# A graph layer as one stream: late rows and root parts beside the first half of the block steps, tiles finished one by one beside the second half

## The chip, the core and the metric

The kernel runs on one core of a Trainium2 chip. The metric is the time of one execution on the device, in microseconds (us). The engines of the core are PE (TensorE, matmul), DVE (VectorE), ACT (ScalarE), POOL (GpSimd, which issues the gathers here) and SP (SyncE, which issues the plain transfers).

## The reference

The input is x (1250 rows of 512 numbers) and 41,250 edges sorted by target (20,000 random pairs in both directions, and one loop at every node). Two graph layers run one after the other, then a mixture of experts:

```
def _graph_conv_max(x, src, dst, W_rel, b, W_root):
    agg = jax.ops.segment_max(x[src], dst, num_segments=N)
    agg = jnp.where(jnp.isfinite(agg), agg, 0.0)
    return agg @ W_rel.T + b + x @ W_root.T
...
h = relu(_graph_conv_max(layernorm(x), src, dst, W1_rel, b1, W1_root))
h = relu(_graph_conv_max(h, src, dst, W2_rel, b2, W2_root))
x = x + h
x = x + ffn(layernorm(x))
```

In the ffn, softmax(rows @ Wr) over all rows picks 512 rows for each of 8 experts (top-k); each expert is two matmuls with a gelu between, and its result, times the probability, is added to its rows.

## The kernel before

**Tiles.** The 1250 rows are 10 tiles of 125 rows (one row a partition). A table of all rows lies in DRAM (table_d, one for each layer). The maximum over a node's neighbours is taken in three ways that add up:

- **Block steps** (`block_steps`, L582). For every tile t and every block b of 125 source rows, the first two neighbours of each row that lie in block b are fetched by matmul: one-hot matrices (`ohs`) times the block's rows, which lie in SBUF as three bf16 parts (`xh`). That is 6 matmuls into a PSUM tile `pq` (two buffers), then one DVE maximum of 125x1024 into `acc2` (for b = 0 an ACT copy). 10 x 10 = 100 steps make a layer; after a tile's tenth step its result is folded into `acc`.
- **Own rows** (`own`, L478). Seven more neighbours of each row, by indirect DMA from POOL (`hb<-table_d,nat_i`), 125 rows of 2 KB each, into `hb` (four buffers of four gathers each; `gathers`, L444), joined by DVE maxima (`merged`, L456, `joined`, L659).
- **Late rows** (`late_groups`, L672). Rows with still more neighbours are sorted into ten lists with 34, 15, 12, 11, 9, 8, 7, 5, 4 and 2 neighbours: 107 gathers in 30 groups of up to four (`hb<-table_d,late_i`). Each list's result goes to DRAM (`late_d`, shown as ovf_d) and comes back to its rows by one gather for each tile (`back`, `hb<-ovf_d,slot_i`), which waits until all lists are stored.

**Root parts** (`root_part`, L314): a tile's row times W_root, plus b: read from table_d, transposed on PE, one bias matmul and four 128x512 f32 matmuls, in six pieces; the result goes to root_d in DRAM. **Convolution** (`conv`, L689): the joined maxima, transposed (`turned`), times W_rel, plus the root part by an identity matmul: five f32 matmul pairs in a row.

**Order.** Every engine keeps the order in which the code records its instructions (`InOrder`, L24; this is why nearly all rows of the profile carry the line L34, and groups are told apart by their tiles). So the order of the loops below is the order of each engine's queue, and an engine that waits holds up all that it has behind it.

A layer is two phases. `first_phase` (L612) runs the block steps with the 60 root pieces spread over all 100 steps, and spreads groups of gathers over them: a group's gathers are recorded ahead, its merge when a computed number of steps is done (`due`). In layer 0 these are the 30 late groups and the own groups of tile 3 (tiles 0 to 2 were joined earlier); in layer 1 the late groups and those of tiles 0 to 3. `second_phase` (L723) has no block steps: own rows of tiles 4 to 9, the back gathers four tiles at a time, and for every two tiles the transposes, convolution and end of tile. The end of a tile in layer 0 is `hidden` (L696): relu, store to the next table, split into the three bf16 parts. In layer 1 it is `residual` (L704): relu and add x, layernorm, store, transpose into `yT`, router logits. Five block steps of layer 1 stand in layer 0's second phase (`begun`, L794), when `xh` of the first five blocks is ready.

The expert part (`Routing`, L1169, and `expert_choice`, L1346) begins with some of expert 0's first matmuls, done for all rows (`dense_steps`, L1285, in three cuts of 4, 3 and 3 tiles, the first two kept in PSUM until the softmax is done), and finds the threshold of the 512 best rows in eight rounds (L1420), each a count on DVE, a small matmul `pn` and a step.

Of the kernel before, what the change touches and what calls it, by code (L numbers as in the profile page):

```python
# [18 lines left out]
P = 128  # L19
# [22 lines left out]
def fast_gnn(tc, ctx, sh, io, y_d):  # L42
# [154 lines left out]
    def load_root(layer):  # L197
        wroot = gw.tile([P, KC, D], F32, name="wroot", bufs=1)
        sp.dma_start(wroot, io[f"w{layer + 1}_root_t"].rearrange("(c p) n -> p c n", p=P))
        brow = gw.tile([1, D], F32, name="brow", bufs=1)  # L200
        sp.dma_start(brow, io[f"b{layer + 1}"])
        weights[layer][:2] = wroot, brow
# [111 lines left out]
    def root_part(layer, t):  # L314
# [3 lines left out]
        turned(rows_ahead.pop(t)[:TN], hT)  # L318
        if t + 3 < NT:
            fetch_row(layer, t + 3)  # L320
        else:
            fetch_root(layer, t + 3 - NT)
# [161 lines left out]
    EARLY = 4  # L484
# [120 lines left out]
    ROOT_PIECES = 2 + KC  # L605
    BEFORE = 4
# [5 lines left out]
    def first_phase(layer, lead, groups, lists, blocks, done):  # L612

        roots = in_turn([root_part(layer, t) for t in range(NT)])
        n_steps, given = NT * NB, 0
        def step():
            nonlocal done, given
            if layer == 0 and done % NB == 4 and done // NB + 2 < NT:  # L620
                onehots(done // NB + 2)
            if layer == 0 and done == NB + 2:
                own_early(2)
            next(blocks)
            done += 1
            while given < done * ROOT_PIECES * NT // n_steps:
                next(roots, None)
                given += 1
            next(blocks)

        while done < lead:
            step()
        for n, (rows, i, fresh, whole) in enumerate(groups):
            due = lead + BEFORE + (n_steps - lead - BEFORE) * n // len(groups)
# [7 lines left out]
            while done < due:  # L642
                step()
# [10 lines left out]
        while done < n_steps:  # L654
            step()
        for _ in roots:
            pass
# [4 lines left out]

    def own_groups(layer, tiles):
        groups = []
        for t in tiles:
            parts_ = grouped(own(layer, t))
            for k, rows in enumerate(parts_):
                whole = (lambda aw, both, t=t: joined(aw, t)) if k + 1 == len(parts_) else None
                groups.append((rows, None, k == 0, whole))
        return groups  # L670
# [24 lines left out]

    def hidden(t, pm):  # L696
        row = gk.tile([P, D], F32, name="line", bufs=LINES)
        act.activation(row[:TN], pm[:TN], AF.Relu)
        stored(table_d[1][t * BR:t * BR + BN, :], row)
        fetch_root(0, t + 3)  # L700
        r1 = gk.tile([P, D], F32, name="line", bufs=LINES)
        yield from parts(t, row[:TN], r1[:TN])

    def residual(t, pm):  # L704
        xt = x_tiles[t % 6]
        fetch_root(1, t + 3)
        fetch_x(t + 3)
        yield
        dve.scalar_tensor_tensor(acc[:TN, t, :], pm[:TN], 0.0, xt[:TN], op0=ALU.max, op1=ALU.add)
        moments(t)  # L710
        spread(t, t + 1)
        yield
        inverted(t, t + 1)
        yn = gk.tile([P, D], F32, name="line", bufs=LINES)
        normed(t, yn[:TN])
        stored(y_d[t * TN:(t + 1) * TN, :], yn)
        yield
        turned(yn[:TN], yT[:, :, t * TN:(t + 1) * TN])
        yield
        head.logits(t, ps_t.tile([P, KC, P], F32, name="pt").rearrange("p c n -> p (c n)"))  # L720
        yield

    def second_phase(layer, finish, beside):  # L723

        going, turns = [], {}

        def on():
            for g in list(going):  # L730
                if next(g, True):
                    going.remove(g)

        def own_rest(t):
            aw = wide()
            for k, rows in enumerate(grouped(own(layer, t))):
                merged(gathers(rows), aw, k == 0)
            joined(aw, t)

        def backs(tiles):  # L740
            hb, _ = gathers([(late_d, slot_i[:, t:t + 1]) for t in tiles])
            for k, t in enumerate(tiles):
                dve.tensor_max(acc[:TN, t, :], acc[:TN, t, :], hb[:TN, k, :])

        def turn(t):
            turns[t] = gk.tile([P, KC, TN], F32, name="turn", bufs=3)
            turned(acc[:TN, t, :], turns[t])

        def ended(*tiles):
            for t in tiles:  # L750
                if t not in turns:
                    turn(t)
                if t + 1 in ready:
                    turn(t + 1)
                g = finish(t, conv(layer, t, turns.pop(t)))
                next(g)
                on()
                going.append(g)

        own_rest(4)  # L760
        backs((0, 1, 2, 3))
        ready = (0, 1, 2, 3)
        own_rest(5)
        ended(0, 1)
        own_rest(6)
        ended(2, 3)
        backs((4, 5, 6, 7))
        ready = (4, 5, 6, 7)
        own_rest(7)
        ended(4, 5)  # L770
        own_rest(8)
        ended(6, 7)
        own_rest(9)
        beside()
        backs((8, 9))
        ready = (8, 9)
        if layer == 1:
            head.constants()
            head.begin(4)
        ended(8, 9)  # L780
        while going:
            on()
            if layer == 1:
                head.begin(1)

    first_phase(0, 6, late_groups(0) + own_groups(0, range(KEPT, EARLY)), set(),
                block_steps(set(range(KEPT))), 0)
# [3 lines left out]
    ready_steps = 5  # L791
    blocks = block_steps(set())

    def begun():  # L794
        load_root(1)
        for _ in range(2 * ready_steps):
            next(blocks)

    second_phase(0, hidden, begun)
    for t in range(3):  # L800
        fetch_row(1, t)
    first_phase(1, 10, late_groups(1) + own_groups(1, range(EARLY)), set(range(NT)), blocks, ready_steps)

    head = Routing(tc, sh, ohs.rearrange("p t n -> p (t n)").bitcast(F32)[:, KC * N:],
                   xh.rearrange("p t k d -> p (t k d)").bitcast(F32), yT)
    head.wide = lambda: ps_q.tile([P, R, D], F32, name="pq")
    x_tiles = [head.left[:, k * D:(k + 1) * D] for k in range(6)]

    def fetch_x(t):
        if t < NT:  # L810
            sp.dma_start(x_tiles[t % 6][:TN], x[t * TN:(t + 1) * TN, :])

    for t in range(3):
        fetch_x(t)
    second_phase(1, residual, lambda: None)
# [353 lines left out]
class Routing:  # L1169
# [4 lines left out]
    def __init__(self, tc, sh, spare, spare2, yT):  # L1174
# [10 lines left out]
        def take(n, dtype=F32, of=spare):  # L1185
# [8 lines left out]
        self.prob = take(N)  # L1194
        self.tops = take(NT)
        self.sm = take(4)
        self.alike = take(P)
# [10 lines left out]
        self.dense = [(take(KC * F).rearrange("p (c f) -> p c f", c=KC),  # L1208
                       take(FC * D).rearrange("p (c d) -> p c d", c=FC)) for e in range(DENSE)]

        self.left = spare[:, self.taken:]
# [4 lines left out]
        self.waiting = []  # L1216
        self.steps = self.dense_steps()
        sp.dma_start(self.wr_s, sh["wr"].rearrange("(c p) e -> p c e", p=P))

    @staticmethod  # L1220
    def words(sh):
# [3 lines left out]
        return (KC * E + KC * P + N + NT + 4 + P + E + 9 + 2 * CC + 3 * P // 2 + NT * E * 5 // 2 + E * FC  # L1225
                + DENSE * (KC * F + FC * D)), FC * N + DENSE * NT * D

    def constants(self):
        dve, act, pe, pool, sp = self.engines
        fw1, fw2 = self.sh["fw1"], self.sh["fw2"]  # L1230
        E, R = fw1.shape[0], self.R
        NT = len(self.sh["rows"])
        sp.dma_start(self.fb1_s, self.sh["fb1_t"])
        for e, (w1, w2) in enumerate(self.dense):
            sp.dma_start(w1, fw1[e].rearrange("(c p) f -> p c f", p=P))
            sp.dma_start(w2, fw2[e].rearrange("(c p) d -> p c d", p=P))
# [30 lines left out]
    def logits(self, t, pl):  # L1267
# [7 lines left out]
        for c in range(KC):  # L1275
            pe.matmul(pl[:, :r], self.wr_rep[:, c].rearrange("p e r -> p (e r)"),
                      self.yT[:, c, t * TN:t * TN + r], start=(c == 0), stop=(c == KC - 1))
        act.copy(self.prob[:, t * TN:t * TN + r], pl[:, :r])
# [6 lines left out]
    def dense_steps(self):  # L1285
# [6 lines left out]
        for e in range(DENSE):  # L1292
            w1, w2 = self.dense[e]
            for n, (t0, t1) in enumerate(zip(cuts, cuts[1:])):
                c0, w = t0 * TN, sum(rows[t0:t1])
                early = e == 0 and n < 2
                if early:
                    both = self.wide()
                for f in range(FC):
                    ph = both[:, f, :] if early else self.bank()  # L1300
# [20 lines left out]
    def softmax(self):  # L1321
# [9 lines left out]
        self.begin(8)  # L1331
# [3 lines left out]
    def begin(self, n):  # L1335

        for _ in range(n):
            if len(self.waiting) < 2 * self.FC:
                next(self.steps)
# [6 lines left out]
def expert_choice(tc, ctx, sh, xs, yT, y_d, out, head):  # L1346
# [73 lines left out]
    for i, shift in enumerate(SHIFTS):  # L1420
# [7 lines left out]
        if i == 0:  # L1428

            for t in range(NT):  # L1430
# [4 lines left out]
        else:  # L1435
# [195 lines left out]
def gnn_expert_choice_kernel(  # L1631
# [49 lines left out]
    with tc.For_i(0, n_again, 1):  # L1681
        with ExitStack() as st:
# [3 lines left out]
            first, second = (spool.tile([P, n], F32, name=f"spare{k}") for k, n in enumerate(Routing.words(both)))  # L1686
            head = Routing(tc, both, first, second, yT)
            head.constants()
            with tc.tile_pool(name="lps", bufs=2, space=PSUM) as lps:
                for t in range(len(both["rows"])):  # L1690
                    head.logits(t, lps.tile([P, D], F32, name="pl"))
                head.wide = lambda: lps.tile([P, 2, D], F32, name="pw")
# [50 lines left out]
```

## Time and profile before

| | us |
|---|---|
| median of 9 runs (lowest, highest) | 922.07 (918.48, 927.66) |
| the profiled execution | 919.23 |
| its span in the profile | 917.4 |
| set-up, to the first late gather | 0 to 113.1 |
| layer 0, first phase | 113.1 to 318 |
| layer 0, second phase, to the first gather of layer 1 | 318 to 399.8 |
| layer 1, first phase | 399.8 to 610.4 |
| layer 1, second phase, to the last logits | 610.4 to 721 |
| softmax, threshold, experts | 721 to 917.4 |

The busy shares over the span are PE 78%, DVE 69%, POOL 56%, ACT 17%. The borders in the table are read from the timeline: 113.1 and 399.8 are the first late gather of each layer, 318 and 610.4 the last fold of each layer's block steps, 721 the last maximum over the logits. A row of the timeline gives the start, the time from the first start to the last end of the merged instructions, the engine, the operation with its output and inputs, the count, and in brackets how long the engine had been idle and what ended that.

### The profile page before, as it was taken

To read this page: it belongs to the slowest core of one execution; us is meant where nothing else is said; L and a number is where in the kernel's file an instruction comes from. 1 tells how busy PE (TensorE), PEld (TensorE's weight loads), DVE (VectorE), ACT (ScalarE), POOL (GpSimd) and SP (SyncE) were. 2 spreads that over 40 slices of the span, in tenths; PEclk is the share of its full clock that TensorE was granted. 3 is DMA by queue.
4 is the path that set the end of the run, shared out by engine and by line. 5 is a ranking of instruction groups with operands and counts; after the bars stand their busy time and mean duration, and the time that the engine had idled before them with its cause. 6 is when DMAs were issued, how large, how long until landed. Compare 5 with 4: busy or idle time off the path is not lost. (4 is left out here: it accounts for less than half of the span.)

```text
span 917.4 us, 8453 instructions
## 1 busy us (share of the span) xinstructions
PE 715.9 (78%) x2554; PEld 377.2 (41%) x2554; DVE 630.2 (69%) x1154; ACT 158.6 (17%) x283; POOL 517.3 (56%) x535
## 2 busy tenths in 40 slices
PE   0193568898989798679888899858859588999992
PEld 0141334454545443335444445433434444444440
DVE  6899489998998866528998989997541565233210
ACT  0641000000000133120000101000311612212110
POOL 6544777776556677046777677777710301466542
PEclk9997879999999989789998999988969889999997
DMA  7587568877667678356877877778850504677753
GB/s 187 160 245 205 137 194 173 212 209 245 188 209 211 209 230 279 130 162 184 182 248 235 267 232 233 229 216 253 261 183 11 174 0 158 140 185 173 136 101 49
DMA packets 70376, 170.57 MB, mean 186 GB/s; under 512 B 13014, under 2 KB 17684, under 8 KB 70322
## 3 DMA queue, kind: packets, MB, share of 16 engines
q0 software_dynamic: 37472, 114.19, 46.8%
q1 hardware_dynamic: 32030, 54.66, 18.9%
q10 hardware_dynamic: 820, 1.10, 0.5%
q8 instruction: 22, 0.36, 0.2%
q14 instruction: 32, 0.26, 0.1%
HBM read 141.46 MB, written 28.40 MB: 185 GB/s over the span
## 5 line engine op out<-in xcount | busy, mean ns | idle before, releaser
L34 PE MATMUL pq<-xh,ohs 126*125 126x512 bf16 x1200 | 296.6, 391 | 64.2 <-DVE acc L34 62.3
L34 POOL DMA_INDIRECT hb<-table_d,late_i x214 | 226.4, 1058 | 131.4 <-issue 51.9
L34 PEld LDWEIGHTS <-ohs 126*125 126x125 bf16 (+1 forms) x1221 | 167.0, 139 | 217.0 <-issue 145.1
L34 DVE TENSOR_TENSOR acc<-acc,pq 125x1024 f32<-125x1024 f32 x180 | 219.2, 1218 | 47.6 <-PE pq L34 41.0
L34 POOL DMA_INDIRECT hb<-table_d,nat_i x140 | 145.6, 1040 | 60.6 <-issue 34.7
L34 PE MATMUL pm<-wrel,turn 128*125 128x512 f32 x160 | 81.4, 656 | 8.9 <-DVE acc L34 6.3
L34 PE MATMUL pm<-wroot,turn 128*125 128x512 f32 x160 | 86.7, 624 | 0.0
L34 ACT COPY acc<-pq 125x1024 f32<-125x1024 f32 x20 | 20.3, 1014 | 357.0 <-PE pq L34 357.0
L34 DVE TENSOR_TENSOR wide<-wide,hb 125x1024 f32<-125x1024 f32 (+1 forms) x60 | 71.4, 1190 | 1.8
L34 POOL DMA_INDIRECT ysel<-y_d,idx x28 | 27.6, 988 | 75.1 <-issue 32.0
L34 DVE TENSOR_TENSOR hb<-hb 125x1024 f32<-125x1024 f32 (+2 forms) x55 | 52.6, 957 | 17.9 <-DMA hb<-table_d,nat_i 17.9
L34 POOL DMA_INDIRECT out<-oo,idx x28 | 44.8, 1600 | 15.8 <-DVE oo L34 8.1
L34 PE MATMUL pm<-yselT,w 128*128 128x512 f32 x112 | 49.9, 599 | 4.7 <-ACT yselT L34 4.7
L34 PE MATMUL pm<-w,hT 128*128 128x512 f32 x112 | 52.7, 591 | 0.0
L34 PEld LDWEIGHTS pm<-wrel,turn 128*125 128x125 f32 x160 | 31.8, 208 | 48.0 <-issue 39.6
L34 DVE TENSOR_TENSOR wide<-hb 125x1024 f32<-125x1024 f32 (+1 forms) x40 | 48.0, 1199 | 5.1 <-DMA hb<-table_d,nat_i 5.0
L34 DVE TENSOR_SCALAR oo<-pm,val 128x512 f32<-128x512 f32 x28 | 21.0, 751 | 44.0 <-PE pm L34 44.0
L34 PEld LDWEIGHTS pm<-wroot,turn 128*125 128x125 f32 x160 | 31.8, 199 | 11.0 <-issue 2.5
L34 ACT COPY turn<-pt 128x500 f32<-128x500 f32 x40 | 22.8, 574 | 68.0 <-PE pt L34 67.7
L34 DVE COPY got<-pi 128x20 f32<-128x20 f32 x7 | 1.2, 178 | 47.7 <-PE pi L34 47.7
L34 PEld LDWEIGHTS pm<-yselT,w 128*128 128x128 f32 x112 | 20.7, 190 | 29.8 <-issue 23.4
L34 DVE TENSOR_REDUCE ohs<-ohs 128x1 f32<-128x125 f32 (+1 forms) x11 | 3.0, 272 | 41.1 <-ACT ohs L34 41.1
(236 smaller groups left out, 785.7 us busy)
## 6 DMA issues: line engine op xcount, KB each, us to landing
w<-in_fw SPq DMA_DIRECT2D x14, 512.0 KB
ohs<-idx_d SPq DMA_DIRECT2D x10, 615.2 KB
ahead<-table_d SPq DMA_DIRECT2D x20, 250.0 KB
root_d<-line SPq DMA_DIRECT2D x20, 250.0 KB
ahead<-root_d SPq DMA_DIRECT2D x20, 250.0 KB
ovf_d<-line SPq DMA_DIRECT2D x18, 224.0 KB
hb<-table_d,late_i POOLq DMA_INDIRECT x214, 6.0
ohs<-in_x SPq DMA_DIRECT2D x10, 250.0 KB
```

The lines of the kernel that those rows point to most:

```text
L34: made = call(*args, **kwargs)
```

## The change

- **Blocks** is now a class that holds a layer's 100 steps and its root pieces. The root pieces are spread over the first `during` steps only: 50 in layer 0, 55 in layer 1 (there from the steps already done on).
- **first_part** takes the place of first_phase: lead steps (8 in layer 0, before 6), then the 30 late groups alone, spread over the steps up to `during`. No own groups are in it.
- **last_part** takes the place of second_phase. It counts ticks. Each tick records one block step (as long as there are any; after that a piece of other work, `beside`), then starts a tile if its start tick has come, and records one piece of every tile begun: merge of its first four gathers; merge of the other four (the back gather is one of them) and join; a tick with nothing; transposes; convolution; and the end of the tile in one to five further pieces. A tile's eight gathers are recorded when the tile before it starts. The start ticks are 0, 4, 7, 10, 14, 20, 26, 32, 38, 43 in layer 0 (tile 3 first, then 0, 1, 2, 4 and on) and 0, 4, 9, 13, 17, 22, 26, 30, 35, 39 in layer 1.
- The split into bf16 parts leaves `hidden`. It is done for all ten tiles by `next_layer`, after layer 0's last block step, with up to nine steps of layer 1 between.
- In layer 1 the root parts read the hidden rows from `acc` in SBUF rather than from DRAM.
- W_root lies in another pool, and its place is used for expert 0's weights after layer 1's root parts; these are loaded at tick 0 of layer 1's last part. x, the router's weights and its constants move to other places with later loads; three x tiles are held where there were six.
- All three cuts of expert 0's first matmuls are now made before the softmax, one half column at a time in ticks without block steps. The ten transposes of the probabilities move from the threshold's round 0 to rounds 1 and 2 (five each), in which no such matmuls stand now.

The core of the diff:

```
     def root_part(layer, t):
...
-        turned(rows_ahead.pop(t)[:TN], hT)
-        if t + 3 < NT:
+        turned(rows_ahead.pop(t)[:TN] if layer == 0 else acc[:TN, t, :], hT)
+        if layer == 0 and t + 3 < NT:
             fetch_row(layer, t + 3)
-        else:
-            fetch_root(layer, t + 3 - NT)
+        elif t + 3 >= NT:
+            fetch_root(layer, order[layer][t + 3 - NT])
...
+        def step(self, roots=True):
...
+            next(self.steps)
+            self.done += 1
+            while roots and self.given < (self.done - self.base) * ROOT_PIECES * NT // (self.during - self.base):
+                next(self.roots, None)
+                self.given += 1
+            next(self.steps)
...
+    def first_part(layer, blocks, lists):
+        groups = late_groups(layer)
+        lead = blocks.done + BEFORE
+        if layer:
+            blocks.base = blocks.done
         for n, (rows, i, fresh, whole) in enumerate(groups):
-            due = lead + BEFORE + (n_steps - lead - BEFORE) * n // len(groups)
+            due = lead + (blocks.during - lead) * n // len(groups)
...
     def hidden(t, pm):
-        row = gk.tile([P, D], F32, name="line", bufs=LINES)
-        act.activation(row[:TN], pm[:TN], AF.Relu)
-        stored(table_d[1][t * BR:t * BR + BN, :], row)
-        fetch_root(0, t + 3)
-        r1 = gk.tile([P, D], F32, name="line", bufs=LINES)
-        yield from parts(t, row[:TN], r1[:TN])
+        act.activation(acc[:TN, t, :], pm[:TN], AF.Relu)
+        stored(table_d[1][t * BR:t * BR + BN, :], acc[:, t, :])
+        ready.add(t)
+        yield
...
+        def tile_work(k):
+            t = order[layer][k]
+            got = fetched.pop(t)
+            if layer == 0 and t < KEPT:
+                dve.tensor_max(acc[:TN, t, :], acc[:TN, t, :], got[0][:TN, t, :])
+            else:
+                aw = wide()
+                merged(got[0], aw, True)
+                yield
+                merged(got[1], aw, False)
+                while blocks.done < (t + 1) * NB:
+                    yield
+                joined(aw, t)
+            yield
+            if not blocks.over():
+                yield
+            hT = gk.tile([P, KC, TN], F32, name="turn", bufs=3)
+            turned(acc[:TN, t, :], hT)
+            yield
+            pm = conv(layer, t, hT)
+            if k + 3 < NT:
+                fetch_root(layer, order[layer][k + 3])
+            yield
+            yield from finish(t, pm)
+
+        fetch(0)
+        begun = tick = 0
+        while begun < NT or going:
+            if not blocks.over():
+                blocks.step(roots=False)
+            else:
+                beside()
+            if tick in at:
+                at[tick]()
+            if begun < NT and tick >= starts[begun]:
+                fetch(begun + 1)
+                going.append(tile_work(begun))
+                begun += 1
             for g in list(going):
                 if next(g, True):
                     going.remove(g)
+            tick += 1
...
+    first = Blocks(0, set(range(KEPT)), 50)
...
+            second = Blocks(1, set(), 55)
+        for t, g in splits.items():
+            if next(g, True):
+                whole.add(t)
...
+        if second.done < NB - 1 and second.done in whole:
+            second.step(roots=False)
...
+    last_part(0, first, (0, 4, 7, 10, 14, 20, 26, 32, 38, 43), hidden, {5: lambda: load_root(1)}, next_layer)
+    while len(whole) < NT:
+        next_layer()
+    first_part(1, second, set(range(NT)))
...
+    last_part(1, second, (0, 4, 9, 13, 17, 22, 26, 30, 35, 39), residual, {0: head.load_dense, 5: begun}, dense)
     head.softmax()
...
-        if i == 0:
-            for t in range(NT):
+        if i in (1, 2):
+            for t in range(NT // 2) if i == 1 else range(NT // 2, NT):
...
-        else:
+        elif i:
             beside()
```

## The prediction

> **What bounds the kernel now.** First the busy time of each engine by stage (columns: stretch, its length, then busy us and count of PE, PEld, DVE, ACT, POOL, then PE's clock, DMA share, GB/s); the stretches are those of the table above.
>
> ```profile
> 113.10:318.00 204.90, 175.33 (x684) 97.19 (x683) 187.01 (x209) 19.28 (x28) 136.20 (x129) 0.96 0.73 206
> 318.00:399.80 81.80, 63.86 (x176) 30.22 (x176) 49.24 (x65) 23.91 (x41) 39.62 (x37) 0.90 0.62 191
> 399.80:610.40 210.60, 185.03 (x704) 101.09 (x704) 184.50 (x172) 19.65 (x29) 155.08 (x149) 0.96 0.77 227
> 610.40:721.00 110.60, 86.19 (x291) 47.17 (x292) 56.08 (x122) 23.44 (x55) 47.08 (x63) 0.86 0.54 171
> ```
>
> In the first phases DVE is busy 91% and 88%, PE 86% and 88%: both are the bound, and their queues mesh. The second phases have no full engine: PE 78%, DVE 60% and 51%. They are what the change goes for: 82 + 111 us in which block steps could run.
>
> Second, the timeline, for how far PE runs ahead of DVE:
>
> ```profile
> 604.51 1.02 PE L34 MATMUL pm<-wroot,turn 128*125 128x512 f32 x2
> ...
> 605.79 0.69 DVE L34 TENSOR_TENSOR acc<-acc,wide 125x512 f32<-125x512 f32 x1
> ...
> 606.40 2.54 DVE L34 TENSOR_TENSOR acc<-acc,pq 125x1024 f32<-125x1024 f32 x2
> ...
> 607.67 1.46 PE L34 MATMUL pq<-xh,ohs 126*125 126x512 bf16 x6 [2.13 <-DVE acc L34]
> ```
>
> PE stands idle 2.13 us until the first of two maxima (606.40 + 1.22) is done: with two pq buffers PE is at most two steps ahead, and while DVE joins own rows PE stops. Third, the price of a gap in PE:
>
> ```profile
> 376.97 5.23 PE L34 MATMUL pq<-xh,ohs 126*125 126x512 bf16 x12 [4.49 <-DVE acc L34]
> ...
> 391.50 3.60 PE L34 MATMUL pm<-wrel,turn 128*125 128x512 f32 x8
> 394.94 1.02 PE L34 MATMUL pm<-ahead,ident 125*125 125x512 f32 x2
> 395.80 0.38 PE L34 MATMUL pq<-xh,ohs 126*125 126x512 bf16 x1
> ```
>
> Twelve step matmuls take 5.23 us after a gap of 4.49, and 2.75 elsewhere (415.88). A convolution is 395.80 - 391.50 = 4.3 us of PE in one piece.
>
> **Prices from rows.** Block step on PE 2.75/2 less overlap = 1.30; maximum on DVE 1.22, 1.27 to the next. Merge of the first four gathers 1.26, of the second four 2.5 (two operations), fold and join 0.7 each. Four transposes 0.45 and ACT copy 0.6; end of tile in layer 1 on DVE 0.69 + 0.69 + 0.18 + 0.15 = 1.8 with gaps, then 0.35, ACT 0.8; logits 0.9. Gathers: 1.25 back to back in quiet stretches (399.81, 401.06); in 560 to 600, 31 in 40 us, so 1.29. I take 1.30; the mean busy of 1.058 plus 0.30 of issue, 1.36, is the upper end.
>
> **First parts.** 107 late gathers now have 38 steps (layer 0) and 42 (layer 1), where 114 and 135 had some 90. POOL needs 107 x 1.30 = 139 us. PE there: 42 steps x 1.30 + ten root parts x 4.7 (five pairs of 0.86 and the transposes) = 102; DVE some 125 (layer 0: 38 maxima, 60 us of late merges, lists, one-hots). So **POOL becomes the bound**, which it was not. The layer 0 part starts at 113.1 as before: the two more lead steps fill a 7.25 us wait of DVE for the lists. POOL ends at 252. Then the last gather must land (6.3), be merged and stored, and the back gather of the first tile waits for that store, lands (6.4) and is merged at tick 1: 11 us until tick 0 in effect, 263.
>
> **Last part of layer 0.** I walk one tile at six ticks' spacing through the two queues, time from the first maximum. DVE: max 0 to 1.25, merge to 2.5, max to 3.8, merge to 6.2, join to 7.6, two max to 10.1. PE: third step at 1.3, fourth at 3.8 (each frees with a maximum two before), transposes wait for the join, 7.6; fifth step waits for a maximum, 8.9 to 10.2; convolution to 14.5; then two steps to 17.1, and DVE, idle since 11.7 but for one maximum, starts the next tile at **17.3**. Work was 12.5 on either engine: the join stops PE 3 us and the convolution stops DVE 4. The first 14 ticks (cheap tiles 0 to 2) take 42 us, four tiles 69, the last five-tick one 16, then seven maxima, merges and the join of tile 9, 15, transposes to relu 6: 148. Stored 3.2 us later (as 396.6 to 399.81 now), the gathers of layer 1 start at 263 + 148 + 3 = 414, now 399.8: **+14**.
>
> **The seam.** Ten splits (20 subtractions of 0.69) and eight maxima, with four lead steps, hold DVE until about 440; POOL has filled its four buffers at 414 + 21 = 435 and waits 5, as it now does at 424.35 (4.83). So 414 + 5 + 139 + 11 = 569 at tick 0 of layer 1's last part.
>
> **Last part of layer 1.** A loop carries it: maximum, end of the tile before (1.8), merge 2.5, join 1.4, maximum, 0.35, ACT normalization 0.8: 9.5; then on PE its transposes and the tile's own 0.9, step 1.3, logits 0.9, convolution 4.3, step 1.3 and the way to DVE: 9.1. **18.6** at four ticks, where PE has 11.3 of work and DVE 12.7. Walking all start ticks (five-tick rounds 23 to 25, the four-tick rounds after them 13) sets ticks 9, 22, 35 at 34, 89, 146, and 39 at 160; tile 9 then needs its steps, join, transposes, convolution between halves of expert 0's columns, normalization and logits: 34. So 569 + 194 = 763, now 721: **+42**. Before, the same 45 steps cost 45 x 2.2 and the second phase 111, together 210 with four tiles' own rows in the steps: the stream saves some 16 there, and the crammed first part has spent three times that.
>
> **Routing and gaps.** In the second threshold round pn waits behind ten transposes: 728.35 to 736.38 is 8.0, later rounds 2.57. Split in two they hide mostly under the count (1.5): -4. Expert 0's third cut, 8 half columns of which about five are left, delays the first pn by 1 to 2: net -2, taken between -6 and +6. The weights of expert 0, for which PE waited 7.56 at 686.86, come at tick 0: hidden behind forty ticks. The walk above ran PE at full clock, but it has gaps of 4 to 7 us in nearly every layer 1 round, beyond those that slowed the rows above (3.35 before 636.82 already did: 5.37 for the eight wrel matmuls against 3.60). Cost of one: 5.37 - 3.60 = 1.8, up to 2.5 from the twelve. I count it for about half of nine rounds, +8, because a cold stretch can fall where DVE is the later one; none and 22 are the ends.
>
> The Trainium skill, "TensorE: Matmul & The Clock Gate", section "HAM oscillation — how this bites in real kernels", warns against PE gaps over about 3.4 us, which then recur each round; that speaks against this order, in which a join and a convolution alternate. Its section "What's actually happening" puts the ramp at under 1% of a typical kernel's span; by that the term would be at most 9 us here, by the rows up to 22, and the trace shows for itself that a gap of 2.13 us costs nothing and one of 4.49 does.
>
> **Sum** against the profiled execution, 919.2: +42 (which holds layer 0's +14) - 2 + 8 = 967; the median of the runs lies 2.8 above the profiled one, so **969**. Bounds: gathers at 1.25 give -5 a layer, at 1.36 +6; gaps 0 or 22.
>
> **Rivals.**
>
> *Rival 1, faster: the queues mesh as in the first phase.* If the stream runs with 9% stalls (DVE 187 of 205), layer 0's last part is PE's 50 x 1.30 + 47 = 112, /0.91 = 123, and 9 of tail: gathers at 398. Layer 1: 398 + 155 + (45 x 1.30 + 60 + 9 of early columns)/0.91 + 12 = 705. That is -16, routing -2: 901, with the median 904. For it: second phases at 60% DVE. Against: the 4.3 us convolution in one piece and two pq buffers. It decides from rounds some 3 us shorter than my walk (15.5 for 18.2, 14.5 for 17.3): fifteen rounds x 3 = 45.
>
> *Rival 2, slower still: gaps keep PE cold and transfers slow POOL.* Every gap costs 2.5 (22), gathers take 1.36 (+13): 969 + 14 + 13 = 996. For it: DMA is busy 83% in 620 to 660, and PE waited 2.93 for a root row at 663. Against: fewer other transfers a microsecond.
>
> *Rival 3: it does what it says, and comes out even.* Gathers at 1.25 and rounds of 16: -11 - 30 = 928. It is the middle between the forecast and rival 1; it holds all of "no change".
>
> **Chances.** Forecast (945 to 982) 0.46; rival 1 (885 to 919) 0.25; rival 2 (over 982) 0.17; rival 3 (919 to 945) 0.12, of which 0.04 lies within 0.3% of 922, about what a measurement of this kernel can tell from no change. So faster 0.25, same 0.04, slower 0.71. Leaving out a tenth on either side, the range is 900 to 992; both signs hold much, and the forecast's own range is 945 to 982.
>
> **What would show it.** Late gathers of layer 0 ending near 252 with POOL hardly waiting; the first of layer 1 near 414; own gathers of layer 1 spread over some 180 us; in the last parts PE idle "<-DVE acc" and "<-ACT line" and DVE idle "<-PE pq", about 4 us each a tile; PE's clock under 0.9 there. Wrong if layer 1's logits come every 15 us or less (rival 1), or if late gathers wait for DVE and the first parts exceed 150 us.

## The result

The changed kernel takes **1022.38 us** (median), the kernel before 921.68: a ratio of 1.1088, 95% interval 1.1068 to 1.1107. The forecast was 969: the direction was right, the size only half of it. The profiled execution spans 1023.3 us, before 917.4: +106, where the working gave +48.

First the busy time of the engines by stage, after (columns as in the first fence of the prediction). The borders are: first and last late gather of layer 0, first back gather, then the same for layer 1, last logits, end.

```profile
115.00:270.60 155.60, 112.37 (x330) 55.70 (x328) 113.36 (x140) 12.95 (x20) 115.41 (x107) 0.81 0.79 219
270.60:285.30 14.70, 10.47 (x34) 5.32 (x34) 8.24 (x10) 0.59 (x1) 6.85 (x8) 0.88 0.79 256
285.30:454.10 168.80, 135.52 (x455) 72.69 (x454) 101.02 (x101) 22.48 (x35) 53.42 (x53) 0.88 0.39 115
454.10:605.70 151.60, 124.52 (x415) 62.72 (x413) 116.87 (x113) 20.27 (x33) 115.86 (x107) 0.89 0.76 217
605.70:623.10 17.40, 16.34 (x64) 8.72 (x62) 12.83 (x14) 2.43 (x4) 7.07 (x7) 1.00 0.84 267
623.10:825.40 202.30, 146.30 (x533) 86.70 (x534) 120.39 (x174) 28.88 (x58) 82.01 (x98) 0.84 0.45 132
825.40:1023.30 197.90, 160.22 (x556) 78.85 (x554) 66.80 (x164) 41.95 (x76) 77.45 (x66) 0.92 0.55 124
```

By these columns no stage has a full engine but the short one at 605. In the first parts PE is busy 72% and 82%, DVE 73% and 77%, POOL 74% and 76%; before, DVE had 91% and 88% in the first phases. But POOL's column leaves out the 0.30 us between one gather and the next: 115.4 + 106 x 0.30 = 147 of 155.6 us in layer 0, and 148 of 151.6 in layer 1, so POOL sets the length of the first parts. In the last parts PE has 80% and 72% at clocks of 0.88 and 0.84, DVE 60%. The idle time has been spread over the layer, not filled. Three groups of the page tell whom the engines wait for (busy time, mean ns of one | idle time before them and what ended most of it):

```profile
L34 DVE TENSOR_TENSOR acc<-acc,pq 125x1024 f32<-125x1024 f32 x180 | 219.1, 1217 | 141.5 <-PE pq L34 137.3
...
L34 POOL DMA_INDIRECT hb<-table_d,nat_i x140 | 143.3, 1024 | 154.7 <-DVE wide L34 87.6
...
L34 PE MATMUL pt<-ident,line 125*128 125x125 f32 x40 | 9.7, 389 | 43.1 <-ACT line L34 43.1
```

DVE's wait ahead of the maxima was 47.6 before. POOL does not pace the own gathers of the last parts: it waits 87.6 us for DVE's merges into `wide`, which free the buffers of the gathered rows. One round of layer 1's last part shows how (timeline: start, duration, what, idle time before and its releaser):

```profile
700.64 0.68 DVE L34 SCALAR_TENSOR_TENSOR acc<-pm,ohs 125x512 f32<-125x512 f32 x1
...
705.72 0.69 DVE L34 TENSOR_TENSOR acc<-acc,wide 125x512 f32<-125x512 f32 x1
...
707.85 0.81 ACT L34 ACTIVATE line<-acc,shift,rstd 125x512 f32<-125x512 f32 x1 [5.16 <-DVE shift L34]
...
708.72 1.10 PE L34 MATMUL pt<-ident,line 125*128 125x125 f32 x4 [6.49 <-ACT line L34]
...
710.44 2.77 PE L34 MATMUL pq<-xh,ohs 126*125 126x512 bf16 x6
...
713.24 1.22 DVE L34 TENSOR_TENSOR acc<-acc,pq 125x1024 f32<-125x1024 f32 x1 [4.30 <-PE pq L34]
...
714.12 3.60 PE L34 MATMUL pm<-wrel,turn 128*125 128x512 f32 x8
...
719.91 1.22 DVE L34 TENSOR_TENSOR acc<-acc,pq 125x1024 f32<-125x1024 f32 x1 [5.01 <-PE pq L34]
```

DVE ends one tile, merges and joins the next (700.64 to 706.4) and takes two maxima; PE stands 6.49 us, until ACT has the normalized row (707.85 to 708.66). Then PE, by now slow (six matmuls in 2.77 instead of 1.46), transposes and convolves, and DVE stands 4.30 and 5.01. The next end of a tile is at 721.05: a round of 20.4.

### The profile page after: what moved, and what is told of

Same layout as the page of the kernel before. It is cut to its first block, busy times and chain, and to the rows that moved or that the text cites. A ratio compares the mean times of both kernels' runs of the same rounds, so it can differ in the third digit from the quotient of the medians.

```text
span 1023.3 us, 8361 instructions
## 1 busy us (share of the span) xinstructions
PE 765.1 (75%) x2554; PEld 400.3 (39%) x2554; DVE 627.4 (61%) x1137; ACT 161.1 (16%) x283; POOL 518.9 (51%) x535
## 5 line engine op out<-in xcount | busy, mean ns | idle before, releaser
L34 PE MATMUL pq<-xh,ohs 126*125 126x512 bf16 x1200 | 335.3, 425 | 83.6 <-DVE acc L34 77.5
L34 POOL DMA_INDIRECT hb<-table_d,late_i x214 | 231.4, 1081 | 130.5 <-issue 55.1
L34 PEld LDWEIGHTS <-ohs 126*125 126x125 bf16 (+1 forms) x1221 | 179.3, 150 | 251.7 <-issue 185.2
L34 POOL DMA_INDIRECT hb<-table_d,nat_i x140 | 143.3, 1024 | 154.7 <-DVE wide L34 87.6
L34 DVE TENSOR_TENSOR hb<-hb 125x1024 f32<-125x1024 f32 (+2 forms) x55 | 61.9, 1125 | 54.4 <-DMA hb<-table_d,late_i 37.7
L34 PE MATMUL pm<-wroot,turn 128*125 128x512 f32 x160 | 90.1, 667 | 0.0
L34 PE MATMUL pt<-ident,acc 125*128 125x125 f32 x120 | 23.3, 328 | 37.5 <-DVE acc L34 35.8
L34 ACT COPY line<-pm 125x512 f32<-125x512 f32 x20 | 11.7, 586 | 235.4 <-PE pm L34 222.0
L34 PEld LDWEIGHTS pm<-wroot,turn 128*125 128x125 f32 x160 | 34.9, 219 | 22.6 <-issue 16.3
L34 PE MATMUL pt<-ident,line 125*128 125x125 f32 x40 | 9.7, 389 | 43.1 <-ACT line L34 43.1
L34 PEld LDWEIGHTS pt<-ident,acc 125*128 125x128 f32 x120 | 17.6, 171 | 45.3 <-DVE acc L34 41.9
```

The costliest lines, as they stand in the source:

```text
L34: made = call(*args, **kwargs)
```

## The experiments

Theory A: in the last parts join and convolution take turns in the two in-order queues. Theory B: the first parts, with POOL's gathers and their landing, carry the loss. Theory C: the cold clock does. Theory D, formed from the busy shares above: the split is the loss; the first parts have room for more block steps. The first four runs stood beside a kernel before at 920.06.

**Convolution in pieces** (layer 0 and 1):

```
-            pm = conv(layer, t, hT)
+            pm = ps_m.tile([P, D], F32, name="pm")
+            for c in range(KC):
+                pe.matmul(...)
+                if c % 2:
+                    yield
+            pe.matmul(pm[:TN], ident[:TN, :TN], ahead.pop(t)[:TN], start=False, stop=True)
```

> The changed kernel, only that the four wrel matmul pairs of a convolution and the root row's come in pieces of 2, 2 and 1 with a block step between, in both last parts. Theory A (turns: in the last parts the join stops TensorE and the 4.3 us convolution stops VectorE, so both add to every round): VectorE gets its next maximum 2.5 to 4 us earlier in each of the 17 full rounds, so 1022 falls by 35 to 55, to 967 to 987; the last parts take 168.8 -> about 145 and 202.3 -> about 175. Theory B (first parts: POOL's gathers and their landing carry the loss, the last parts are bound by what lands): within 6 of 1022. Theory C (cold clock: rounds are long because the clock is at 0.84 to 0.88 there): the gaps shrink but stay over 2.5 us, so little changes, 1010 to 1025.

991.04, ratio 1.0763 (1.0608 to 1.0918): -31 us, just short of theory A's -35 to -55, far from B and C. Layer 1 from its last late gather to the last logits gave 25 of it (220.0 to 195.3), layer 0 from its last late gather on 6 (183.4 to 177.7); the first parts stayed (156.4 and 149.2, after 155.7 and 151.6).

**Transposes of the normalized row a tick later** (one `yield` more ahead of `turned(yn...)` in `residual`):

> The changed kernel, only that the transposes of the normalized rows in layer 1 come one tick later, with a block step in the wait (TensorE waited 43.1 us in 9 rounds for ScalarE's normalization there). Theory A (turns in in-order queues): TensorE does a step in that wait; about 2.5 to 4.5 us less in each of 9 rounds, 995 to 1000; layer 0 stays as it is. Rival within it: the wait moves to the next maximum or to the join (VectorE then waits for the step behind the transposes), within 6 of 1022. Theory B (first parts): within 3 of 1022, less the one tick more that the last tile takes.

1011.58, ratio 1.0986 (1.0829 to 1.1142): -11, half of what A gave it and more than its rival. Layer 1's last part fell by 7. The wait removed was largely taken over by the next one in the same loop: in layer 1's last part PE's 43.1 us for ACT are gone, but its waits for DVE ahead of the maxima's transposes grew from 10.9 to 29.6, ahead of the steps from 0.4 to 13.5.

**75 steps beside the late rows:**

```
-    first = Blocks(0, set(range(KEPT)), 50)
+    first = Blocks(0, set(range(KEPT)), 75)
...
-            second = Blocks(1, set(), 55)
+            second = Blocks(1, set(), 75)
...
-    last_part(0, first, (0, 4, 7, 10, 14, 20, 26, 32, 38, 43), ...
+    last_part(0, first, (0, 3, 5, 7, 9, 12, 15, 18, 21, 24), ...
...
-    last_part(1, second, (0, 4, 9, 13, 17, 22, 26, 30, 35, 39), ...
+    last_part(1, second, (0, 2, 5, 7, 10, 12, 15, 17, 20, 23), ...
```

> The changed kernel with 75 instead of 50 and 55 block steps beside the late rows, the tiles of the last parts starting every 2 to 3 ticks. First parts have TensorE busy 112 of 155.6 and 124 of 151.6 us and VectorE 113 and 117, so 25 and 20 more steps (1.3 and 1.25 each) would fill them to 145 and 143. Theory D (the split is the loss: the first parts hold these steps at no more than 5 us each, the last parts lose 45 of 95 steps): last parts of 110 to 130 and 160 to 175 instead of 168.8 and 202.3, together 915 to 950. Theory A alone (join and convolution carry a round however many steps it holds): first parts +10 each, rounds 3 to 4 us shorter, 965 to 990. Theory B (first parts already crammed: VectorE waits there for landing gathers and each step more costs about 2.2 as before the change): the first parts grow by 50 each or nearly, 1000 to 1030.

887.43, ratio 0.9638 (0.9498 to 0.9777): -135, more than theory D gave, and faster than the kernel before. In this kernel tile 0's root part of layer 1 is made from its maxima instead of its row; the runs below with 75 steps keep the row. The first parts did not grow: 149.6 and 149.1 between first and last late gather, after 155.7 and 151.6.

**Two of three terms in a step** (`range(3)` to `range(2)` in `block_steps`):

> The changed kernel with the third of the three bf16 terms of the rows left out of every block step (four matmuls instead of six), so the maxima lack the lowest bits. Theory A (turns): a step lies once or twice in each round's chain, 0.45 us less warm and 0.9 cold; 19 rounds: -9 to -30, 990 to 1013. If TensorE were simply too slow in the last parts (theory C, cold clock, in full), 50 and 45 steps of 0.45 to 0.9 go: -45 to -80, 940 to 977. Theory B (first parts by POOL): first parts unchanged within 4 us by all of them.

1005.44, ratio 1.0919 (1.0753 to 1.1086): -17, theory A's range; a third less work in every step did little (at a lower clock, 0.836 for 0.874), so PE's speed as such is not the bound. The first parts stayed (153.2 and 152.8).

**Four runs on a chip on which the kernel before took 988.58**: only ratios count here. 75 steps with the rows in order (`blocks.base = blocks.done - 3`, x and expert 0's weights at tick 0); with it the pieces and the later transposes; 100 steps and starts every second tick; and that with pieces and transposes.

> 75 block steps beside the late rows in both layers as in the run before, with layer 1's root parts starting three steps earlier, so that tile 0's row is transposed before its maxima replace it (in the run before it was taken after), and x and expert 0's weights fetched at tick 0. Theory D (the 45 steps were free in the first parts, since TensorE and VectorE stood idle there, and 2.4 to 3.3 us each in the last parts): the same time as the run before, 880 to 892, faster than the kernel before the change by 3 to 4%. If the reading of the row after its maxima had taken a wait away: 892 to 905.

> The run with 75 steps in order, and with it the convolution in pieces of 2, 2 and 1 and the normalized row's transposes one tick later. Theory A as a part beside D (turns still cost in the last parts of 104.7 and 136.3 us, where TensorE is busy 84% and 82%): another 8 to 20 us less, 865 to 880. If tiles started every 2 to 3 ticks already lay join beside convolution: within 6 of the run with 75 steps.

> All 100 block steps beside the late rows, none in the last parts; tiles start every second tick. Theory D at its end: the first parts are now bound by TensorE and VectorE (92 steps of 1.3 and 47 us of root parts: about 170; the run with 75 had 168.2 and 167.2 up to the first back gather), so 25 steps more cost 1.5 to 2.2 each there, +38 to +55 a layer, and the last parts lose 25 steps of 1.3 to 2.4 but are then bound by the own gathers (83 x 1.3 = 108 us): 900 to 935, slower than 75. If steps in a last part cost the 2.4 to 3.3 that the first 45 cost: 830 to 870.

> All 100 block steps beside the late rows, with the convolution in pieces and the later transposes. With no steps in the last parts the pieces have nothing to come between: within 6 of the run without them, by every theory.

0.9808 (0.9578 to 1.0037), 0.9718 (0.9540 to 0.9896), 0.9870 (0.9689 to 1.0050) and 0.9870 (0.9685 to 1.0055). The intervals are wide and overlap: the dial is flat from 75 to 100 as far as these runs tell. With 100, the late gathers take 182.6 and 179.0 (with 75 on this chip 160.6 and 165.2), and the parts after them are shorter by 18 and 9: given with one hand, taken with the other. POOL is no longer the bound of the first parts there: beyond the 0.30 us between gathers it stood 42 and 37 us, in layer 0 mostly for DVE's merges (28.5). That the pieces do nothing where no step is left came as expected (969.0 and 969.0).

**Steps first, tiles after** (50 and 55 steps as in the change; starts at 50, 52, ... and 45, 47, ...):

> The changed kernel with its 50 and 55 steps beside the late rows, but the tiles of a last part start only when its 50 or 45 steps are done, then every second tick: steps and tiles are not interleaved at all. Theory A (turns: interleaved at this spacing, join and convolution stop both queues): 50 steps alone take 50 x 1.4 = 70 and ten tiles without steps about 95 and 120, so last parts of 165 to 175 and 190 to 200 with the wait for the back gather hidden behind the steps, against 183 and 220: 975 to 1000, faster than the interleaved order. If interleaving did save anything beside 168.8 and 202.3: 1025 to 1060.

980.62, ratio 1.0664 (1.0614 to 1.0715), within theory A's range: not interleaving at all is 42 us faster than interleaving at this spacing, 31 of it in layer 1 from the last late gather to the last logits, 8 in layer 0 from the last late gather on. Steps alone, then tiles alone, for both layers (same columns):

```profile
286.30:356.00 69.70, 66.98 (x291) 39.03 (x289) 59.41 (x52) 4.43 (x5) 7.91 (x8) 1.00 0.16 52
356.00:446.00 90.00, 67.69 (x193) 32.01 (x194) 57.39 (x66) 22.12 (x41) 47.97 (x44) 0.91 0.59 174
610.20:675.00 64.80, 55.91 (x240) 32.66 (x239) 55.65 (x59) 4.62 (x5) 16.75 (x33) 0.95 0.22 69
675.00:781.60 106.60, 84.79 (x292) 47.10 (x291) 64.38 (x117) 23.12 (x53) 67.11 (x65) 0.90 0.66 207
```

Fifty steps by themselves take 69.7, some 1.39 each, with PE busy 96% at full clock.

**Convolution beside the next join.** Same steps, same starts; two lines:

```
             turned(acc[:TN, t, :], hT)
             yield
+            while k + 1 < NT and tick < starts[k + 1] + 1:
+                yield
             pm = conv(layer, t, hT)
```

> The changed kernel with all as it is (50 and 55 steps, the same start ticks), only that a tile's convolution waits until the tick in which the next tile's second merge and join are issued, so that TensorE convolves while VectorE joins (as it falls out by itself in the run with 75 steps and starts every third tick). Theory A (turns): a round loses about the convolution's 4.3 us or the join's 3.9 us, up to 16 rounds: 950 to 985. Theory D in its narrow form (the number of steps left in the last parts makes the loss, wherever the convolution lies): within 10 of 1022.

950.54, ratio 1.0337 (1.0284 to 1.0391): **-72 from two lines that move no work between stages**, theory A's range, against theory D in its narrow form. The round in its timeline:

```profile
675.77 0.65 PE L34 MATMUL pt<-ident,line 125*128 125x125 f32 x4 [2.61 <-ACT line L34]
...
680.09 3.60 PE L34 MATMUL pm<-wrel,turn 128*125 128x512 f32 x8
...
680.79 1.22 DVE L34 TENSOR_TENSOR hb<-hb 125x1024 f32<-125x1024 f32 x1
...
682.04 1.23 DVE L34 TENSOR_TENSOR wide<-wide,hb 125x1024 f32<-125x1024 f32 x1
...
683.53 1.02 PE L34 MATMUL pm<-ahead,ident 125*125 125x512 f32 x2
...
684.02 0.69 DVE L34 TENSOR_TENSOR acc<-acc,wide 125x512 f32<-125x512 f32 x1
```

Merge and join (680.79 to 684.71) now lie beside the convolution (680.09 to 684.4). PE's wait for ScalarE fell from 43.1 to 19.8. Ends of tiles in layer 1 follow every 14.9 us on average, after 19.5. The two last parts of it (back gather to next layer's gathers, and to the logits):

```profile
287.50:420.20 132.70, 118.83 (x442) 65.52 (x441) 99.07 (x98) 21.36 (x34) 53.84 (x52) 0.95 0.48 144
591.10:755.70 164.60, 134.12 (x540) 78.90 (x540) 119.71 (x176) 27.84 (x58) 83.04 (x98) 0.94 0.53 164
```

Of the 73.8 us saved here (371.1 - 297.3), 28.9 is PE's own busy time for nearly the same work (281.8 - 252.9; 988 and 982 matmuls), as its clock went from 0.88 and 0.84 to 0.95 and 0.94; 44.9 is PE's idle time. So theory C has a part, but as a consequence of the gaps: only the order was changed.

**75 steps again, alone and with pieces and later transposes**, beside a kernel before at 919.72:

> The same kernel as the run with 75 steps in order, on another chip or in other conditions: the run on the chip where the kernel before took 989 had a ratio of 0.981, the first one 0.964. Expected 0.960 to 0.980, 885 to 900 where the kernel before takes 920.

> The same kernel as the run with 75 steps, pieces and later transposes: it was 1% below the run with 75 steps on the slower chip. Theory A beside D: 8 to 14 us below the run with 75 steps alone, 0.950 to 0.970 of the kernel before. If the first was chance: within 4 of it.

889.89, ratio 0.9686 (0.9648 to 0.9725), and **884.00, ratio 0.9631** (0.9599 to 0.9664), the fastest kernel found. The second is 6 below the first, less than expected, and the intervals touch. Stages of the first (late gathers, hand-over to the first back gather, and last part, of each layer):

```profile
111.70:264.30 152.60, 126.38 (x454) 67.97 (x454) 136.98 (x160) 14.02 (x20) 115.59 (x107) 0.92 0.81 228
264.30:282.70 18.40, 18.24 (x75) 10.01 (x74) 16.18 (x19) 2.76 (x4) 7.28 (x8) 1.00 0.72 217
282.70:386.70 104.00, 87.68 (x299) 45.81 (x297) 71.42 (x74) 19.89 (x34) 53.77 (x52) 0.93 0.60 183
386.70:536.70 150.00, 133.68 (x508) 71.63 (x509) 133.58 (x127) 21.19 (x33) 114.90 (x107) 0.99 0.76 220
536.70:554.90 18.20, 17.95 (x71) 9.97 (x71) 14.53 (x16) 2.76 (x4) 7.26 (x7) 1.00 0.70 210
554.90:690.40 135.50, 108.82 (x426) 61.68 (x425) 99.97 (x159) 25.56 (x56) 86.31 (x97) 0.94 0.65 203
```

The first parts are about as long as with 50 and 55 steps (152.6 and 150.0, after 155.7 and 151.6), with DVE at 90% and 89%; POOL's gathers and the 0.30 us between them fill 147 us of each, as in the changed kernel. What the steps filled is seen in DVE's waits of layer 0's first part (total us, times, longest), in the changed kernel and then with 75 steps:

```profile
DVE hb L34 <- DMA hb<-table_d,late_i: 22.2, 12, 4.7
DVE wide L34 <- DMA hb<-table_d,late_i: 16.2, 5, 5.7
```

```profile
DVE hb L34 <- DMA hb<-table_d,late_i: 6.5, 6, 2.2
...
DVE wide L34 <- DMA hb<-table_d,late_i: 1.1, 2, 0.9
```

**How the two causes share**: 62 and 75 steps, each with the convolution beside the join (62: starts 0, 3, 5, 7, 10, 15, 20, 25, 30, 35 and 0, 3, 7, 11, 15, 19, 23, 27, 31, 35).

> 62 block steps beside the late rows in both layers, tiles every 4 to 5 ticks, and the convolution waiting for the tick of the next tile's join. If steps beside the late rows are free up to where TensorE and VectorE fill there (busy 112 to 128 of 156 us with 50 and 55), and in the last parts, now bound by TensorE (119 of 133 and 134 of 165 us), cost 1.3 to 1.6 each: 19 steps are 25 to 30 us, 918 to 928. If the split no longer costs once the convolution lies beside the join: 940 to 955. If each step costs as before the alignment (2.4 and 3.3 us): 895 to 905.

> 75 block steps beside the late rows and the convolution waiting for the tick of the next tile's join. With starts every 2 to 3 ticks the convolution fell beside the next tile's merges anyway, so the wait moves it by a tick at most: 880 to 892, within 6 of the run with 75 steps alone. If alignment and split add: 850 to 870.

931.28, ratio 1.0113 (1.0082 to 1.0143), and 892.20, ratio 0.9666 (0.9608 to 0.9725). The first lies between its two ranges, 918 to 928 and 940 to 955, nearer the one in which a step costs its own price. From 50 and 55 to 62 that is 19 steps for 19 us, and 26 more for 39: 1.0 and 1.5 each, near the 1.39 of a step by itself. Of the 132 us that the run with 75 steps gained on the changed kernel, some 72 are then the alignment and some 60 the 45 steps. This is an estimate, since the start ticks differ between these runs too. At 75 with starts every 2 to 3 ticks the alignment adds nothing, as expected: it comes with the starts.

## Why the prediction was half right

The time fell into rival 2's range (over 982, chance 0.17). The deviation of 58 us (+106 for +48), by the prediction's own milestones (tick 0 "in effect" is read at DVE's first merge with a back gather, 294.9 and 629.4; the prediction meant a tick before it, so about 2.5 us of its +26 in each layer belong to the rows below):

| step | forecast | measured | deviation |
|---|---|---|---|
| first late gather of layer 0 | 113.1 | 115.0 | +2 |
| late gathers, layer 0 and 1 | 139, 144 | 155.7, 151.6 | +24 |
| last late gather to tick 0 "in effect" | 11, 11 | 24.2, 23.7 | +26 |
| layer 0, tick 0 to layer 1's gathers | 151 | 159.2 | +8 |
| layer 1, tick 0 to last logits | 194 | 196 | +2 |
| clock, counted apart | 8 | in the row above | -8 |
| routing | -2 | +1.5 | +4 |

So 50 of the 58 us lie in the first parts and the hand-overs, theory B's place, while the runs above won their time in the last parts.

- **"POOL needs 107 x 1.30 = 139 us"** failed in its price, not in the engine. POOL did become the bound: its gathers kept it busy 1.08 us each (115.4 / 107; 116.0 in layer 1), with 0.30 to the next, so 1.38 for 1.30, above the 1.36 that the prediction called the upper end. Two rows of layer 0, a longer gather and the one long wait inside the stage:

```profile
129.26 0.94 POOL L34 DMA_INDIRECT hb<-table_d,late_i  x1 [4.58 <-DVE lov L34]
...
153.16 1.85 POOL L34 DMA_INDIRECT hb<-table_d,late_i  x1 [0.30 <-issue]
```

 Of the +24, the price is 17 (147 and 148 for 139 twice); the rest is waiting, 8 us in layer 0, over half of it this wait for a late list, and 4 in layer 1, where 5 were forecast. DVE stood 38.4 us in layer 0 for landing gathers, because with few steps between them an in-order merge reaches its rows before they have landed, and PE then waited for DVE; but that did not set the length. With 75 steps 7.6 us of these waits are left and the stage still takes 152.6, and every first part with 50 to 75 steps took 147 to 156 us where the kernel before took about 920. Whether POOL itself or the DMA engines behind it (busy 79% and 76%) stretched the gathers was not tried. The prediction's sign of being wrong, first parts over 150, came; its reason, late gathers that wait for DVE, came in small part only.
- **"11 us until tick 0 in effect"** failed: the landing of a store was not in it, and the last gathers' way to the store took longer. Layer 1:

```profile
604.60 1.06 POOL L34 DMA_INDIRECT hb<-table_d,late_i  x1 [0.30 <-issue]
...
612.07 0.68 DVE L34 TENSOR_TENSOR wide<-hb 125x512 f32<-125x512 f32 x1
...
613.09 1.06 SPq L34 DMA_DIRECT2D ovf_d<-wide  x2
...
623.12 0.95 POOL L34 DMA_INDIRECT hb<-ovf_d,slot_i  x1 [8.26 <-DMA ohs<-in_x]
...
629.37 1.27 DVE L34 TENSOR_TENSOR hb<-hb 125x1024 f32<-125x1024 f32 x1 [8.01 <-DMA hb<-ovf_d,slot_i]
```

 From the last gather's issue to the store 8.5, from the store to the back gather 10.0, its landing 6.3; in layer 0 these are 10.3, 5.3 and 9.5. The releaser named in layer 1 is x's load, issued in between; whether it or the store was the later one was not tried. Nor was the hand-over changed by itself: in layer 1 PE was busy 16.3 of the 17.4 us up to the back gather with steps and root pieces left over from the first part. With 75 steps the way to the back gather is as long (18.4 and 18.2), but PE is busy nearly all of it (18.2 and 18.0).
- **The walk of layer 1's last part** held: 196 for 194. Its loop through both queues is the one that the runs cut open (pieces, later transposes, convolution beside the join), and its sum came out, with rounds more even (17.6 to 22.8) than the 13 to 25 forecast. In part that is chance: the cold clock is inside the 196, and not beside it.
- **The walk of layer 0** was short: rounds of 17.9 to 19.6 for 17.3. It reckoned with full clock, and PE was at 0.88.
- **The clock term**, 8 for half of nine rounds with 22 as the end, was for layer 1 alone. There the same work costs PE 12.2 us more than with shorter gaps (146.3 - 134.1), within its ends and for 7 matmuls fewer; layer 0, where the sum had no such term, had 16.7 (135.5 - 118.8, for 13 matmuls more). The Trainium skill, "TensorE: Matmul & The Clock Gate", warns in "HAM oscillation — how this bites in real kernels" of gaps that recur each round: the trace agrees (0.84 with long gaps, 0.94 with shorter ones). Its figure of under 1% of a span ("What's actually happening") is for the ramp in a typical kernel; with gaps in nearly every round it does not hold here: 28.9 of 1023.3 is 2.8%.
- **Routing**: the transposes split in two saved nothing in sum (197.9 for 196.4). It was not tried alone.
- **Rival 1** named the right condition, queues that mesh, and the right point, rounds 3 us shorter. It is where two lines bring the change (rounds of 12.9 and 14.9), but even then it takes 950, since its price assumed first parts of 139 and hand-overs of 11. **Rival 2** had two of the right terms, gathers of 1.36 and gaps of 22; what its 996 lacked is above all the hand-overs.

What stays open is what stretched the gathers, how much the hand-overs cost by themselves, how the 28.9 of clock and the 44.9 of idle time depend on one another, and how much the two runs with 100 and 75 steps differ on an undisturbed chip.

## What to carry to other kernels

When two in-order queues work on one stream with two buffers between them, write down per tick what each gets: a long piece of one belongs in the tick of the other's long piece, and a round in which they fall into different ticks costs up to their sum. Before work is split between two stages, count in each the idle time of every engine, the waits for landing included, and count the pause between two issues as taken: an engine 74% busy was the bound here. Steps that fill the others' waits were free as long as it stayed the bound, and the same steps elsewhere cost their full price. A hand-over through DRAM costs three landings, gather, store and gather (24 us, twice), and needs independent work left over to lie behind.

## What the runs showed of the hardware

Between 150 and 180 us the indirect gathers kept the DMA engines 93% busy, while all transfers together moved 193 GB/s, and a 125-row gather took 10.9 us (median) to land, 6.0 over the whole kernel; in the kernel before, the same stretch had 8.3, and DVE waited for none of it. An indirect gather kept POOL 0.94 to 1.98 us, three in four under 1, and 0.30 lay between two. Six bf16 matmuls of 512 columns took 1.46 us or, as behind the gap of 6.49 us above, 2.77. One chip ran every kernel some 7% slower than the others (988.58 for 920): late gathers of the same kernel took 165.2 there and 150.0 here in layer 1, and no rows of the trace name the cause.
